# Graph attention and a gated feed-forward net on one core: the edge loop taken out of the scheduler's hands and written in its own order

## The chip, the cores and the metric

The kernel runs on one core of a Trainium2 chip. The core has five engines with a queue each, and each takes its instructions strictly in the order in which the program holds them: TensorE (PE in the profile; its weight loads are a row of their own, PEld), VectorE (DVE), ScalarE (ACT), GpSimd (POOL) and SyncE (SP), which here only starts transfers. Transfers with an index list are started from Pool. The metric is the device time of one execution in microseconds, the median over several; the kernel before has 3848.79 us.

## The reference, cut to what matters

6250 nodes with 256 features, 206,250 edges sorted by their target node `dst`, 64 features an edge. A layer of graph attention with eight heads, then a feed-forward block, then a small mixture of experts, all per node. The part in question is the attention over edges:

```python
q = (x @ Wq.T + bq).reshape(n, HEADS, C)       # k, v likewise
e = (edge_attr @ We.T).reshape(-1, HEADS, C)
k_e = k[src] + e
v_e = v[src] + e
alpha = jnp.sum(q[dst] * k_e, axis=-1) / np.sqrt(C)
amax = jax.ops.segment_max(alpha, dst, num_segments=n)
ex = jnp.exp(alpha - amax[dst])
denom = jax.ops.segment_sum(ex, dst, num_segments=n)
alpha = ex / (denom[dst] + 1e-16)
out = jax.ops.segment_sum(v_e * alpha[..., None], dst, num_segments=n)
...
x = _layernorm(x + h, ln1_g, ln1_b)
h = jax.nn.gelu(x @ W1.T + b1, approximate=False) @ W2.T + b2
return _layernorm(x + h, ln2_g, ln2_b)
```

After it come a gate (softmax, the best two of four experts), four experts and a shared net of three layers, per node, and the sum of them is the output.

## The kernel before

**Stages.** A first stage builds index tables from `dst`. A second computes q, k, v and the skip term for all nodes in 50 blocks of 125 and writes them to `kv_d`, `q_d` and `rn_d` in HBM. Then the edges follow in `sorted_edges`, the branch taken for sorted input; `any_edges` is the branch for other input and does not run here.

**The edge loop.** 403 steps of 512 edges, in four tiles of 128. For step i:
- `load(i)`: four gathers by Pool (line 689) bring the k and v rows of the source nodes into a buffer X, and SP loads the edge features into the same buffer. X has five buffers, and loads are written four steps ahead.
- `score(i)`: TensorE spreads q over the edges (line 705) into two banks `qg`; VectorE multiplies with k (L711) and reduces to one score per head (L713), written into X.
- `turn(i)`: TensorE transposes edge features and scores (L721), ACT copies them out as `xT` (L723).
- `rows(i)`: TensorE multiplies by a small matrix `ws` (L733), which gives scores per target node; VectorE takes their maximum (L737).
- `weigh(i)`: ACT takes the exponentials with that maximum as bias, and their sum (L744).
- `turn_back(i)`: transposes (L752) and a copy `pT` (L754).
- `gather(i)`: sixteen records of products with v and the edge features (L767) into a single bank `op`.
- `keep(i)`: VectorE picks and reduces (L775, L778), ACT copies (L777), SP stores the partial rows `os` to `part_d` (L779).

**Groups.** Every four steps `group(g)` prepares q for four steps: a gather of q rows by Pool (`qq`, L648), a round trip of them through HBM (`qs`, then `qw`, SP), row numbers by SP (`rb`), a comparison on VectorE (`oh`, L671), transposes, products with the edge weights and two copies into `ws` on ACT (L681).

**Nodes.** When all edges of two node blocks are stored, which happens every 16 steps, a generator `ffn(b0, ...)` is appended to `nodes`. It first runs `merge`: four gathers a block by Pool fetch the partial rows (`A`, L788), VectorE joins them (L795 to L821), TensorE applies the edge weights (L825, L832). Then follow the skip gate, a layernorm, the feed-forward block (`h1`, L448 with Gelu L450; `w2`, L459), a second layernorm and the experts (L505 and after). Every `yield` ends a piece. `advance(1)` puts one piece of the first generator into the program; it is called three times in a step.

**What sets the order.** The kernel is written on tiles; a scheduler of the framework orders the instructions of every engine from a cost model of its own and places the waits. The written order is only a priority. One instruction, the load of the scalar table for exponentials behind the Gelus (L451), is pinned to its place. PSUM has eight banks: two for `qg`, two for `m` (transposes and rows), one for `op` and three that turn among groups and nodes.

The loop that writes the steps:

```python
            for i in range(-1 - GQ, B + 2):
                if 0 <= i - 2 < B:
                    keep(i - 2)
                    follow(i - 2)
                if 0 <= i - 1 < B:
                    weigh(i - 1)
                if 0 <= i + 1 < B:
                    score(i + 1)
...
                if 0 <= i + AHEAD < B:
                    load(i + AHEAD)
```

Of the kernel before, what the change touches and what calls it, by code (L numbers as in the profile page):

```python
# [40 lines left out]
def gnn_moe_layer(ctx: ExitStack, tc: tile.TileContext, a: dict, out: bass.AP):  # L41
# [322 lines left out]
    def ffn(b0, p3, bank, attention):  # L364
# [67 lines left out]
        def transposed(v, name):  # L432
            tp = bank([128, 2, M])
            for j in range(n):
                for k in range(2):
                    nc.tensor.transpose(tp[:, k, j * NB : (j + 1) * NB],  # L436
                                        v[:, j, k * 128 : (k + 1) * 128], ident[:NB, :NB])
            vT = p3.tile([128, 2, M], F32, name=name, tag="yT")
            nc.scalar.copy(vT, tp)
            return vT  # L440

        yT = transposed(y, "yT")
# [8 lines left out]
        tc.keep_in_program_order(nc.scalar.preload_act_table_set("natural_log_exp_and_others"))  # L451
# [4 lines left out]
        for j in range(n):  # L456
            ps = bank([NB, D])
            for f in range(FF // 128):
                nc.tensor.matmul(ps, h1[:, f, j * NB : (j + 1) * NB], w2[:, f, :],  # L459
                                 start=(f == 0), stop=(f == FF // 128 - 1))  # L460
                if f == FF // 256 - 1:
# [15 lines left out]
        zT = transposed(z, "zT")  # L477
# [3 lines left out]
        lg = bank([NB, n, NE])  # L481
        for j in range(n):
            for k in range(2):
                nc.tensor.matmul(lg[:, j, :], zT[:, k, j * NB : (j + 1) * NB], gw[:, k, :],  # L484
                                 start=(k == 0), stop=(k == 1))

# [68 lines left out]
        wp = bank([128, NE // 2, M])  # L555
        for j in range(n):
            for g in range(NE // 2):
                nc.tensor.transpose(wp[:, g, j * NB : (j + 1) * NB], wx[:, j, 2 * g : 2 * g + 2].rearrange("p e d -> p (e d)"),
                                    ident[:NB, :NB])
        nc.vector.tensor_tensor(e2, e2, wp, ALU.mult)  # L560
        wt = bank([NE + 1, M])
        for j in range(n):
            nc.tensor.transpose(wt[:, j * NB : (j + 1) * NB], w[:, j, :], ident[:NB, :NB])
        wT = p3.tile([NE + 1, M], F32, name="wT", tag="wT")
        nc.scalar.copy(wT, wt)
        yield
        for j in range(n):
            cs = slice(j * NB, (j + 1) * NB)
            ps = bank([NB, D])
# [3 lines left out]
            nc.tensor.matmul(ps, wT[:, cs], e3b, start=False, stop=True)  # L573
            nc.vector.tensor_tensor(x2[:, j, :], ps, x2[:, j, :], ALU.add)
        yield
        nc.sync.dma_start(rows_of(out), x2)

    def sorted_edges(ctx):
# [50 lines left out]
        with tc.tile_pool(name="fd", bufs=3, space=bass.MemoryType.DRAM) as fd, tc.tile_pool(name="fg", bufs=2) as fg, \  # L629
# [7 lines left out]
                tc.tile_pool(name="f_g", bufs=3, space=PSUM) as f_g:  # L637
            groups = {}
            state = {}

            def bank(shape):
                return f_g.tile(shape, F32, name="gp", tag="gp")

            def group(g):
# [4 lines left out]
                                             in_offset=bass.IndirectOffsetOnAxis(ap=idq[:, g : g + 1], axis=0))  # L649
                yield  # L650
# [14 lines left out]
                yield  # L665
                qw = fg.tile([64, GQ * 2, D], BF16, name="qw")
                for u in range(T // 2):
                    nc.sync.dma_start(qw[32 * u : 32 * u + 3 * W],
                                      qs[64 * u : 64 * (u + 1)].rearrange("(m j) (s d) -> (j s) m d", j=W, s=3))
# [491 lines left out]
```

## Time and profile before

| what | value |
| --- | --- |
| median of 14 runs | 3848.79 us (3832.93 to 3866.11) |
| the profiled execution, its time | 3828.54 us |
| its span, first to last instruction | 3826.8 us |
| granted TensorE clock, mean over the span | 0.763 |
| bytes moved | 727.33 MB, 190 GB/s |
| first score reduce (L713) / last gather product (L767) | 582.9 us / 3692.6 us |

A line of costly groups reads: source line, engine, operation, output and inputs, count, then busy time and mean of one in ns, then the idle time of the engine ahead of these instructions and what ended most of it. A line of waits reads: who waited, for whom, us in total, times, the longest. "issue" stands for time in which nothing that the profile shows was waited for. The clock is given as a share of full speed.

### The profile page before, as it was taken

The page shows a single profiled execution, that of the slowest core. Times are in us where ns is not written, and L with a number is a line of the kernel's source. Part 1 is how long each engine was busy: PE and PEld are TensorE (multiplying, and loading weights), DVE is VectorE, ACT ScalarE, POOL GpSimd, SP SyncE. Part 2 cuts the span into 40 slices and gives each one's busy share as a digit, 9 for nine tenths or more (in the row PEclk, how much of TensorE's full clock was granted, in tenths as well). Part 3 has the DMA queues.
Part 4 walks back from the last instruction along what each step waited for, and adds up shares of the span by engine and source line. Part 5 has one row for each costly group of instructions (what it writes and reads, how often), then busy time and mean ns, then how long its engine had stood idle before and what let it go on. Part 6 is the DMA issues. An engine that isn't in the chain of part 4 may idle for free. (4 is left out here: it accounts for less than half of the span.)

```text
span 3826.8 us, 59098 instructions
## 1 busy us (share of the span) xinstructions
PE 2829.5 (74%) x19362; PEld 1814.8 (47%) x19363; DVE 2401.7 (63%) x5624; ACT 1454.2 (38%) x4313; POOL 1992.7 (52%) x2030
## 2 busy tenths in 40 slices
PE   2566636787777878788888779777878688888866
PEld 2222214454554545455555545554555455555555
DVE  9322225776656756676777567766767677677753
ACT  0111103444434434344444435443434445444442
POOL 0111126766545655656666456655645666567620
PEclk6777767677877777788778867876777778878777
DMA  0233348978667768777878678767866788778730
GB/s 22 102 119 117 116 150 248 269 218 229 199 161 211 208 180 218 218 215 210 229 229 227 179 205 234 219 191 204 234 175 199 223 233 239 200 210 247 221 88 9
DMA packets 611830, 727.33 MB, mean 190 GB/s; under 512 B 384196, under 2 KB 461309, under 8 KB 611514
## 3 DMA queue, kind: packets, MB, share of 16 engines
q0 software_dynamic: 169040, 495.21, 43.7%
q1 hardware_dynamic: 425153, 196.53, 19.8%
q10 hardware_dynamic: 17321, 31.70, 2.3%
q8 instruction: 158, 2.59, 0.3%
q14 instruction: 158, 1.29, 0.1%
HBM read 614.28 MB, written 108.73 MB: 189 GB/s over the span
## 5 line engine op out<-in xcount | busy, mean ns | idle before, releaser
L689 POOL DMA_INDIRECT X<-kv_d,srcT x1612 | 1569.5, 974 | 906.4 <-issue 368.2
L711 DVE TENSOR_TENSOR prod<-qg,X 128x512 f32<-128x512 f32 x806 | 541.3, 682 | 193.1 <-DMA X<-kv_d,srcT 140.5
L713 DVE TENSOR_REDUCE X<-prod 128x32 f32<-128x1024 f32 x403 | 486.6, 1207 | 0.5
L767 PE MATMUL o<-X,pT 128*32 128x192 f32 x6448 | 442.3, 398 | 16.8 <-ACT pT L754 11.6
L705 PE MATMUL qg<-qw,oh 24*128 24x256 bf16 x1612 | 282.2, 314 | 206.8 <-DVE prod L711 193.4
L744 ACT ACTIVATE P<-m,os 128x128 f32<-128x128 f32 x806 | 288.8, 363 | 383.3 <-issue 268.3
L721 PE MATMUL m<-ident,X 128*80 128x128 f32 x1612 | 324.0, 334 | 117.3 <-issue 67.5
L723 ACT COPY xT<-m 80x512 f32<-80x512 f32 x403 | 234.1, 581 | 376.2 <-PE m L721 375.1
L788 POOL DMA_INDIRECT A<-part_d,idp x200 | 255.2, 1276 | 226.3 <-DVE oa L816 102.1
L733 PE MATMUL m<-xT,ws 80*64 80x128 f32 x3224 | 333.9, 336 | 40.7 <-ACT xT L723 37.3
L721 PEld LDWEIGHTS m<-ident,X 128*80 128x80 f32 x1612 | 194.9, 142 | 227.7 <-issue 104.8
L733 PEld LDWEIGHTS m<-xT,ws 80*64 80x64 f32 x3224 | 212.7, 164 | 166.5 <-ACT xT L723 108.1
L752 PE MATMUL m<-ident,P 128*128 128x128 f32 x806 | 208.7, 338 | 88.3 <-ACT P L744 87.5
L767 PEld LDWEIGHTS o<-X,pT 128*32 128x32 f32 x6448 | 194.5, 126 | 165.3 <-issue 69.0
L448 PE MATMUL gp<-yT,w 128*128 128x250 f32 x800 | 236.7, 457 | 41.7 <-ACT h L450 37.0
L737 DVE TENSOR_REDUCE os<-m 128x2 f32<-128x256 f32 x403 | 167.7, 416 | 154.5 <-PE m L733 62.8
L705 PEld LDWEIGHTS <-oh 24*128 24x128 bf16 x1612 | 77.0, 95 | 391.9 <-issue 385.4
L778 DVE TENSOR_REDUCE os<-ov 128x64 f32<-128x256 f32 x403 | 236.6, 587 | 0.1
L299 POOL TENSOR_TENSOR qr<-qt 125x256 f32<-125x256 f32 x50 | 33.4, 669 | 365.0 <-ACT qt L297 345.0
L448 PEld LDWEIGHTS gp<-yT,w 128*128 128x128 f32 x800 | 181.8, 235 | 86.2 <-ACT h L450 40.3
L459 PE MATMUL gp<-w,h 128*125 128x256 f32 x800 | 194.5, 397 | 14.0 <-ACT h L450 13.9
L775 DVE TENSOR_TENSOR ov<-o,hmc 128x256 f32<-128x256 f32 x403 | 167.2, 415 | 54.9 <-PE o L767 54.0
(235 smaller groups left out, 4511.5 us busy)
## 6 DMA issues: line engine op xcount, KB each, us to landing
X<-in_edge_dram SPq DMA_DIRECT2D x403, 128.0 KB
part_d<-os SPq DMA_DIRECT2D x403, 98.0 KB
X<-kv_d,srcT POOLq DMA_INDIRECT x1612
qs<-qq SPq DMA_DIRECT2D x101, 192.0 KB
qw<-qs SPq DMA_DIRECT2D x202, 96.0 KB
q_d<-qt ACTq DMA_DIRECT2D x50, 312.5 KB
rb<-rel_d SPq DMA_DIRECT2D x200, 64.0 KB
rn_d<-rn SPq DMA_DIRECT2D x50, 250.0 KB
```

What stands on the lines that cost most here:

```text
L448: nc.tensor.matmul(ps, w1[:, k, f * 128 : (f + 1) * 128], yT[:, k, :], start=(k == 0), stop=(k == 1))
L689: nc.gpsimd.indirect_dma_start(out=X3[:, t, : 2 * D], out_offset=None, in_=kv_d, in_offset=bass.IndirectOffsetOnAxis(ap=srcT[:, i, t : t + ...
L705: nc.tensor.matmul(qgs[u][:, c, :], oh[rows, 2 * q + c, :], qw[rows, 2 * q + c, :], start=True, stop=True)
L711: nc.vector.tensor_tensor(prod[:, 2 * u : 2 * u + 2, :].rearrange("p t (s c) -> p t s c", s=2), qgs[u].rearrange("p t (s c) -> p t s c", s ...
L713: nc.vector.tensor_reduce(X3[:, :, 2 * D + ED : 2 * D + ED + H], prod.rearrange("p t (h c) -> p t h c", c=C), AX.X, ALU.add)
L721: nc.tensor.transpose(xp[:K, t, :], X3[:, t, 2 * D :], ident)
L723: nc.scalar.copy(xT, xp[:K])
L733: nc.tensor.matmul(sp[(t % 2) * 64 : (t % 2 + 1) * 64, t // 2, :], ws[:, t // 2 * 2 * GQ + 2 * q + t % 2].rearrange("k g w h -> k (g w h)" ...
L744: nc.scalar.activation(P[:, u, :], sp[:, u, :], AF.Exp, bias=os[:, u, PR - 1 : PR], accum_out=os[:, u, PR - 2 : PR - 1])
L767: nc.tensor.matmul(op[32 * r : 32 * (r + 1), u, :].rearrange("p (s c) -> p s c", s=3), pT[:, u, 32 * r : 32 * (r + 1)], va, start=True, st ...
L778: nc.vector.tensor_reduce(os[:, :, 0:C], ov.rearrange("p u h c -> p u c h"), AX.X, ALU.add)
L788: nc.gpsimd.indirect_dma_start(out=A[:, s, i * (H // 2 * PR) : (i + 1) * (H // 2 * PR)], out_offset=None, in_=part_d[: 2 * W * tiles_to(b0 ...
```

## The change

The edge branch gets `tc.manual_schedule()`: inside it every engine's instructions stand in the order in which the program writes them, and the scheduler only places the waits. The loop is rewritten with it:

- `weigh(i)` stands at the end of step i, behind the maximum of `rows(i)`, and no longer at the head of step i + 1.
- `keep` is split. The product and the reduce on VectorE stay at the head of the step; the copy on ACT and the store (`store`) follow the transposes.
- A group runs in six passes and begins seven steps ahead of its first use. All open groups move on by a pass in every step, ahead of `turn`.
- The gathers of partial rows leave `merge` and become `fetch`, begun two steps after the store of the last row needed, two gathers a step, into one buffer for each block of the pair. The node generator is appended six steps later.
- Four pieces of node work a step in place of three; the pieces are cut anew, so that what TensorE writes into a bank is read in the next piece.
- Such banks come from a pool of their own with one buffer, `held`; the turning pool goes from three banks to two.
- The table load behind the Gelus is no longer pinned in this branch. In the other branch both kinds of bank come from one pool of two buffers each.
- The loop runs eight steps longer at its end, without edge work.

```diff
-    def ffn(b0, p3, bank, attention):
+    def ffn(b0, p3, bank, held, attention, pin=True):
...
         def transposed(v, name):
-            tp = bank([128, 2, M])
+            tp = held([128, 2, M])
             for j in range(n):
                 for k in range(2):
                     nc.tensor.transpose(tp[:, k, j * NB : (j + 1) * NB],
                                         v[:, j, k * 128 : (k + 1) * 128], ident[:NB, :NB])
+            yield
             vT = p3.tile([128, 2, M], F32, name=name, tag="yT")
             nc.scalar.copy(vT, tp)
             return vT
...
-        tc.keep_in_program_order(nc.scalar.preload_act_table_set("natural_log_exp_and_others"))
+        ins = nc.scalar.preload_act_table_set("natural_log_exp_and_others")
+        if pin:
+            tc.keep_in_program_order(ins)
...
-            ps = bank([NB, D])
+            ps = held([NB, D])
             for f in range(FF // 128):
                 nc.tensor.matmul(ps, h1[:, f, j * NB : (j + 1) * NB], w2[:, f, :],
                                  start=(f == 0), stop=(f == FF // 128 - 1))
-                if f == FF // 256 - 1:
+                if f % 4 == 3:
                     yield
...
-                tc.tile_pool(name="f_g", bufs=3, space=PSUM) as f_g:
+                tc.tile_pool(name="f_g", bufs=2, space=PSUM) as f_g, \
+                tc.tile_pool(name="f_h", bufs=1, space=PSUM) as f_h, tc.manual_schedule():
...
             def group(g):
...
                                              in_offset=bass.IndirectOffsetOnAxis(ap=idq[:, g : g + 1], axis=0))
                 yield
+                yield
...
                 nc.scalar.copy(qT, tp)
                 yield
+                yield
                 qw = fg.tile([64, GQ * 2, D], BF16, name="qw")
...
+                yield
                 oh = fg.tile([64, GQ * 2, 128], BF16, name="oh")
                 nc.vector.tensor_scalar(oh[:, : 2 * n], rb[:, : 2 * n], j3[:64], None, op0=ALU.is_equal)
-                yield
...
             def keep(i):
-                os, op = state.pop(i)
+                os, op = state[i]
...
+                nc.vector.tensor_reduce(os[:, :, 0:C], ov.rearrange("p u h c -> p u c h"), AX.X, ALU.add)
+
+            def store(i):
+                os, op = state.pop(i)
                 nc.scalar.copy(os[:, :, C : C + ED], op[:, :, 4 * C :])
-                nc.vector.tensor_reduce(os[:, :, 0:C], ov.rearrange("p u h c -> p u c h"), AX.X, ALU.add)
                 nc.sync.dma_start(part_d[2 * W * T * i : 2 * W * T * (i + 1)]
...
-            def merge(b0, n, at):
-                for j in range(n):
-                    A = fm.tile([NB, 2, H * PR], F32, name="A", tag="A")
+            def fetch(b0):
+                rows_of[b0] = []
+                for b in range(b0, min(b0 + 2, NBLK)):
+                    A = fm.tile([NB, 2, H * PR], F32, name="A", tag=f"A{b - b0}")
+                    rows_of[b0].append(A)
                     for s in range(2):
                         for i in range(2):
                             nc.gpsimd.indirect_dma_start(
...
                         yield
-                    for _ in range(4):
-                        yield
+            def merge(b0, n, at):
+                As = rows_of[b0]
+                for j in range(n):
+                    A = As[j]
...
+            def each(steps):
+                for v in list(steps):
+                    if next(v, steps) is steps:
+                        steps.remove(v)
...
-            for i in range(-1 - GQ, B + 2):
-                if i % GQ == GQ - 2 and 0 <= (i + GQ + 2) // GQ < NG or i == -1 - GQ:
-                    prep.append(group(0 if i < -GQ else (i + GQ + 2) // GQ))
+            fetched = []
+            for i in range(-1 - 2 * GQ, B + 10):
+                g, r = divmod(i + 2 * GQ - 1, GQ)
+                if r == 0 and 0 < g < NG or i == -1 - 2 * GQ:
+                    prep.append(group(max(g, 0)))
                 if 0 <= i - 2 < B:
                     keep(i - 2)
-                    follow(i - 2)
-                if 0 <= i - 1 < B:
-                    weigh(i - 1)
                 if 0 <= i + 1 < B:
                     score(i + 1)
+                each(prep)
                 if 0 <= i < B:
                     turn(i)
                 if 0 <= i - 1 < B:
                     turn_back(i - 1)
+                if 0 <= i - 2 < B:
+                    store(i - 2)
                 advance(1)
                 if 0 <= i < B:
                     rows(i)
                 advance(1)
                 if 0 <= i - 1 < B:
                     gather(i - 1)
+                if 0 <= i < B:
+                    weigh(i)
+                advance(1)
                 if 0 <= i + AHEAD < B:
                     load(i + AHEAD)
-                for g in prep[:1]:
-                    if next(g, prep) is prep:
-                        prep.pop(0)
+                fetched += [fetch(b0) for b0 in after(i - 4)]
+                each(fetched)
+                nodes += [ffn(b0, p3, bank, held, merge, pin=False) for b0 in after(i - 10)]
                 advance(1)
             advance(1000)
```

`after(i)` yields the pairs whose last partial row belongs to step i.

## The prediction

> **What bounds the kernel now.** I read the page's busy shares and its 40 slices first, then the costly groups and the waits by engine, then five-microsecond windows through one stall and its timeline, and last the tail.
>
> ```profile
> PE 2829.5 (74%) x19362; PEld 1814.8 (47%) x19363; DVE 2401.7 (63%) x5624; ACT 1454.2 (38%) x4313; POOL 1992.7 (52%) x2030
> L689 POOL DMA_INDIRECT X<-kv_d,srcT x1612 | 1569.5, 974 | 906.4 <-issue 368.2
> L788 POOL DMA_INDIRECT A<-part_d,idp x200 | 255.2, 1276 | 226.3 <-DVE oa L816 102.1
> ```
>
> No engine is full. Pool's gap in front of a gather is 0.30 us where it waits for nothing (368.2/1208), so one costs 0.95 + 0.30 = 1.25 us and a step's four 5.0; with a quarter of a q gather a step needs 5.3 us of Pool at least. The tile's waits and the waits of VectorE say who holds the loop up:
>
> ```profile
> PE qg L705 <- DVE prod L711: 193.4, 121, 12.5
> DVE A L795 <- DMA A<-part_d,idp: 144.8, 22, 10.9
> POOL A L788 <- DVE oa L816: 102.1, 8, 23.0
> DVE t L407 <- DMA rn<-rn_d: 92.9, 11, 12.5
> DVE oh L671 <- DMA rb<-rel_d: 64.4, 13, 14.7
> ```
>
> Three loads (A, rn, rb) arrive late behind an instruction that stands early in VectorE's order: 144.8 + 92.9 + 64.4 = 302 us in which VectorE stands still, and TensorE (qg) and Pool after it. One such stall, in windows (busy of PE, PEld, DVE, ACT, POOL; granted clock, DMA share, GB/s) and in the timeline:
>
> ```profile
> 2115.00:2120.00 5.00, 0.85 (x5) 0.31 (x5) 2.13 (x5) 1.67 (x5) 2.26 (x3) 0.69 1.00 278
> 2120.00:2125.00 5.00, 0.00 (x0) 0.00 (x0) 0.69 (x1) 0.00 (x0) 0.00 (x0) 0.50 0.53 154
> 2125.00:2130.00 5.00, 1.55 (x5) 0.98 (x5) 2.89 (x7) 0.00 (x0) 0.00 (x0) 0.50 0.16 41
> ...
> 2135.00:2140.00 5.00, 5.00 (x29) 4.02 (x28) 3.36 (x9) 1.65 (x4) 0.00 (x0) 1.00 0.00 0
> ```
>
> ```profile
> 2127.00 0.48 DVE L671 TENSOR_SCALAR oh<-rb,j 64x1024 bf16<-64x1024 bf16 x1 [2.28 <-DMA rb<-rel_d]
> 2128.45 0.58 PE L705 MATMUL qg<-qw,oh 24*128 24x256 bf16 x2 [11.88 <-DVE prod L711]
> 2142.16 0.94 POOL L689 DMA_INDIRECT X<-kv_d,srcT  x1 [24.29 <-DVE ln_st L390]
> ```
>
> Everything is dark for 10 us, the clock falls to 0.50, and Pool gets no free X buffer for 24 us. The starts of the 403 reduces L713 in the timeline give the pace: 582.9 for the first, 32 steps to 769.5 (5.83 us each, hardly any node work yet), then 890.2 to 3649.8 for steps 48 to 400, which is 7.84 us a step or 125.4 us per 16 steps, the interval at which node pairs become ready. 44 steps over 13 us hold 833 us. The last gather product ends at 3692.6; the tail is then 134 us.
>
> **The change, part by part.** *Order.* The work is the same; what changes is who stands behind whom. I add up 16 steps (one node pair) by the written order. Start to start in the timeline, a step's edge work is 3.7 us on VectorE (product 2 x 0.61, reduce 1.13, kept rows 0.33 + 0.51, maximum 0.34, the small ones 0.2), and 2.9 us on TensorE at full clock (q 0.35, transposes 0.45 + 0.32, rows 0.59, gather product 0.79, a quarter of the group's 1.6). VectorE and TensorE can drift apart by less than a step (ov needs the last gather product, which needs the ov before it), so the dearer engine sets each step. Four pieces of the node generator fall into a step, 51 pieces in all, so 13 of 16 steps carry some.
> - Merge and layernorm, six steps: pieces of 3.7, 0.3, 3.4, 1.0, 4.8 and 3.9 us on VectorE (512-wide 0.60, 256-wide 0.34, dependent small ones 0.2) make steps of 7.4, 4.3, 7.1, 5.7, 8.5 and 7.6: the fourth adds 1.0 for the transposes that gather waits behind. 40.6 us.
> - Three steps with h1 and w2: the yT transposes 1.1; edge work up to rows 1.1; h1 whole 7.3 (32 records at 0.23, as 16 of L505 took 3.55); rows 0.6, w2 quarter 1.75, gather 0.8, quarter 1.75; then 1.1, 1.75, 0.6, 1.75, 0.8; then VectorE 1.4 + 7.7 and transposes 1.1. With hops about 29.7 us.
> - Four steps of gate and experts, TensorE: 7.7, 7.3, 5.4, 5.0 = 25.4. Pool has to issue four steps of 5.3 plus the next pair's eight A gathers at about 1.55, 33.6 us. An X buffer is filled three steps ahead of its product, so Pool may fall some 8 us behind here; without that cover the step's sum grows by 8.
> - Three steps without node work at Pool's 5.3: 16.
>
> Together 111.7 at full clock.
>
> *The exponentials* (two of 0.36 + 0.20, 0.8 in all) move from the head of step i+1 to the tail of step i. Behind them wait the dense copies of the fourth slot; they were not on the path of the step, and TB(i) a step later has over 2 us in hand: nothing. If that slack is gone, 0.8 a step. *Scalar tables*: 67 + 25 + 23 + 20 = 135 loads of 1.283 become about 50, since Gelu stands in one piece; 85 x 1.28 = 109 us of ACT, an engine at 38%, and I count nothing for it beyond the h1 piece, which no longer waits for them.
> *q groups over six passes*: qs, qw and oh stand two passes behind the DMA that feeds them, some 14 us against landings of about 5 to 8 (qq 7.5 at most to its transpose); oh's 64.4 goes. The two ws copies (2 x 0.62) now stand in ACT's queue ahead of xT in one step of four, and rows waits for xT: 1.2 x 4, half of it in steps that TensorE sets: +2.
> *Partial rows early*: 200 gathers, same number, issued six steps before their merge and into two buffers: 144.8 and Pool's 102.1 go. rn is loaded five steps ahead of its use, now in order: 92.9 goes.
> *Banks*: the turning pool falls from three to two and one bank is held. In h1 a bank is free when Gelu (0.47) and two hops are done, before the next pair of products (0.92) ends: nothing; if not, about 0.5 a product, 4 us per pair.
> [...] If each of the eight products waited out its Gelu, 8 x 0.65 x 25 = 130 us would come on top; no such wait stands in this trace, with three banks.
>
> *Clock.* 16 gather products take 0.86 us at full clock and 1.51 in the slow stretches, so work at half clock costs 0.75 more. L767's mean of 398 ns between 349 and 531 (its median and maximum over 890 to 3650) puts about 27% of the work there now. Steps that VectorE sets leave TensorE idle half the time, so the slow share will not vanish, but the dark stretches go. From both sides: 46 us of TensorE work on the path x 0.75 x 0 to 27% is 0 to 9; I take 12%, +4.
> [...]
>
> **Sum.** 111.7 + 2 + 4 = 118 us per 16 steps. First reduce 583; the first pair enters ten steps later than its rows, so 35 steps at 5.8 = 203; 23 sixteens x 118 = 2714; last steps 13. Tail: the last pair but one has hardly begun (before it was about there too); a pair alone takes 57.5 from 3769.4 to the end and two merges of 9, 76 us; 71 + 76 = 147. Total 583 + 203 + 2714 + 13 + 147 = 3660 in the profiled execution's terms. That execution was 3828.54 (span 3826.8), 20 below the median of 3848.79: 3680.
>
> **The rivals.**
> *A. All waits go and the order costs nothing* (fast): 3828 - 302 = 3526, as a median 3545. For it: from the first reduce to the last are 3093 us, so the other 358 steps average (3093 - 833)/358 = 6.3 us, with node work in them. Against it: the pieces come whole, h1 and half of w2 in one step of 14 us, which a finer mixture avoids.
> *B. Half clock in the heavy pieces* (slower than before). Place: h1 and w2 come right behind two steps of 8 us in which TensorE has 3 us of work, the condition under which windows show 0.50. Price: 46 x 0.75 = 35 us per pair if all of it ran so; at half, 111.7 + 2 + 17 = 131, 946 + 23 x 131 = 3959, median 3980. It decides from 125.3 us per pair, a slow share of a third. Against it: in the windows of 600 to 700, with TensorE two thirds busy, the clock was 0.82.
> *C. Pool takes the place.* Its eight A gathers in four steps are not hidden and the products wait for X: 118 + 8 = 126, 3844, median 3865: next to no change. Against it: three steps of lead, and a Pool that idles in the nine steps before.
> *D. The order isn't what sets the pace*, and part of the stalls moves to X's landing: prod waits 140.5 us for it now; as much again gives 3660 + 140 = 3800, median 3820.
>
> **Numbers.** Forecast (3560 to 3770) 0.60; A or faster 0.16; D 0.08; C 0.05; B 0.11. One can tell 0.3%, 12 us, from no change. Faster is 0.60 + 0.16 + 0.08 less 0.02 of D, whose upper end reaches the border: 0.82. Same is that 0.02 and 0.02 of C: 0.04. Slower is B and the rest of C: 0.14. The range leaves out half of A and nearly all of B: 3490 to 3860.
>
> **What would show it.** VectorE's waits for A, rn and rb near zero; table loads about 50; POOL A no longer waiting for oa; no step over 20 us, one of 13 to 17 per pair; 16 steps in 112 to 123 us; clock over 0.78. It is wrong if qg still waits over 100 us for prod, if rows waits for ws copies over 100 us, or if prod waits over 250 us for X.

## The result, and the profile after

The changed kernel takes 4142.23 us (median of 10 runs, 4130.13 to 4162.67) against 3844.94 us for the kernel before beside it (47 runs): a ratio of 1.0777 with a 95% interval of 1.0752 to 1.0801. It is slower by 7.8%, where 3680 us and "faster" had been predicted. The profiled execution took 4149.3 us, its span is 4147.5 us and the mean granted clock 0.722 (before: 3826.8 us, 0.763).

The span divides as the prediction's sum does, which shows where the miss lies:

| part of the sum | predicted | after |
| --- | --- | --- |
| start to the first reduce | 583 | 577.6 |
| the next 35 steps | 203 | 192.8 |
| the remaining 367 steps | 2714 | 3218.2 |
| last reduce to the end | 160 | 158.9 |

Everything around the loop with node work was right to a few us. Per 16 steps the loop takes 140 us (steps 48 to 400: 139.8), not 118, and 125.4 before. Without node work (the first 32 steps) a step is now 5.3 us, 0.5 less than before.

The engine shares of the changed kernel, then its costly groups and its tile and DMA waits, in the columns explained earlier:

```profile
PE 2862.4 (69%) x19362; PEld 1837.8 (44%) x19363; DVE 2517.8 (61%) x5624; ACT 1344.8 (32%) x4229; POOL 1955.8 (47%) x2030
```

```profile
L704 POOL DMA_INDIRECT X<-kv_d,srcT x1612 | 1548.0, 960 | 1452.7 <-PE o L782 999.1 <-issue 375.4 <-DMA X<-kv_d,srcT 11.2
L449 PE MATMUL gp<-yT,w 128*128 128x250 f32 x800 | 192.5, 396 | 24.7 <-ACT h L451 23.4 <-ACT yT L440 1.3
L782 PE MATMUL o<-X,pT 128*32 128x192 f32 x6448 | 465.3, 421 | 24.4 <-ACT os L796 24.3
```

```profile
POOL X L704 <- PE o L782: 999.1, 187, 18.7
DVE os L752 <- PE m L748: 336.6, 121, 8.0
DVE prod L726 <- PE qg L720: 228.8, 135, 7.2
PE qg L720 <- DMA qw<-qs: 226.1, 74, 11.8
PE gh L436 <- DVE y L429: 159.1, 25, 10.0
PE m L748 <- ACT xT L738: 140.8, 258, 2.0
PE gh L436 <- DVE y L400: 137.0, 25, 6.3
DVE os L752 <- DMA part_d<-os: 125.4, 23, 8.5
PE gp L676 <- DMA qq<-q_d,idq: 89.6, 30, 9.7
```

The most telling number is TensorE's busy time: 2862.4 us against 2829.5, only 33 us more, in a span that grew by 321. TensorE idles 4147.5 - 2862.4 = 1285 us in place of 997. Against the kernel before, then, nearly all of the lost time is waiting and not slower work. The waits for A, rn and rb are gone from VectorE, as predicted; in their place TensorE waits for qw (226 us, 12 before) and for the node values y (296 us, 36 before), and VectorE for the rows (337 us, 63 before). The wait for qq (90 us) was there before (87). Pool's 999 us in front of the X gathers are a symptom: it waits until the gather products have freed an X buffer, so it is ahead of the loop and not what holds it up.

A node pair now takes the same course every time. The intervals between the reduces L728 from step 208 on, in us, show one pair:

```
10.1 4.2 3.8 10.0 7.5 7.5 4.2 14.2 7.7 9.0 8.8 18.2 6.4 8.7 11.7 7.9
```

The 14.2 is a stall that nearly every pair has; over steps 48 to 400 this step takes 13.1 us on average. In the windows (busy of PE, PEld, DVE, ACT, POOL; clock, DMA share, GB/s) and the timeline of the changed kernel:

```profile
2205.00:2210.00 5.00, 0.00 (x0) 0.00 (x0) 0.70 (x4) 0.25 (x1) 2.41 (x3) 0.50 0.95 284
2210.00:2215.00 5.00, 3.85 (x20) 2.39 (x19) 4.86 (x12) 1.94 (x8) 0.00 (x0) 0.50 0.55 160
...
2245.00:2250.00 5.00, 5.00 (x24) 4.11 (x24) 0.00 (x0) 2.54 (x6) 0.00 (x0) 1.00 0.00 0
```

```profile
2191.42 6.95 SPq L683 DMA_DIRECT2D qw<-qs  x2
2198.48 7.15 SPq L797 DMA_DIRECT2D part_d<-os  x1
2209.23 0.43 DVE L752 TENSOR_REDUCE os<-m 128x2 f32<-128x256 f32 x1 [6.72 <-DMA part_d<-os]
2210.70 1.09 PE L720 MATMUL qg<-qw,oh 24*128 24x256 bf16 x4 [8.95 <-DMA qw<-qs]
...
2219.40 0.94 POOL L704 DMA_INDIRECT X<-kv_d,srcT  x1 [11.38 <-PE o L782]
...
2237.08 1.10 PE L436 MATMUL gh<-ident,y 125*128 125x125 f32 x4 [5.92 <-DVE y L429]
```

From 2190 to 2210 the DMA engines' share is 0.88 to 1.01 in windows of 5 us. In that time SyncE needs 6.95 us to issue the two qw copies and then 7.15 us for one store. The q rows arrive after 2210, TensorE stands for 8.95 us in front of its q products with other work written behind them, and VectorE for 6.72 us. At 2237 TensorE stands again, this time for y. In the third window h1 occupies TensorE for 5 us, VectorE does nothing and no DMA runs: one engine is full and ScalarE works 2.54 us, while VectorE, Pool and the DMA are dark.

### The profile page after: what moved, and what is told of

It reads as the page before. It is cut to its first block, busy times and chain, and to the rows that moved or that the text cites. A ratio compares the mean times of both kernels' runs of the same rounds, so it can differ in the third digit from the quotient of the medians.

```text
span 4147.5 us, 59038 instructions
## 1 busy us (share of the span) xinstructions
PE 2862.4 (69%) x19362; PEld 1837.8 (44%) x19363; DVE 2517.8 (61%) x5624; ACT 1344.8 (32%) x4229; POOL 1955.8 (47%) x2030
## 5 line engine op out<-in xcount | busy, mean ns | idle before, releaser
L704 POOL DMA_INDIRECT X<-kv_d,srcT x1612 | 1548.0, 960 | 1452.7 <-PE o L782 999.1
L726 DVE TENSOR_TENSOR prod<-qg,X 128x512 f32<-128x512 f32 x806 | 519.3, 683 | 273.0 <-PE qg L720 228.8
L728 DVE TENSOR_REDUCE X<-prod 128x32 f32<-128x1024 f32 x403 | 491.7, 1220 | 13.9
L782 PE MATMUL o<-X,pT 128*32 128x192 f32 x6448 | 465.3, 421 | 24.4 <-ACT os L796 24.3
L752 DVE TENSOR_REDUCE os<-m 128x2 f32<-128x256 f32 x403 | 169.3, 420 | 463.3 <-PE m L748 336.6
L720 PE MATMUL qg<-qw,oh 24*128 24x256 bf16 x1612 | 229.0, 337 | 262.2 <-DMA qw<-qs 226.1
L736 PE MATMUL m<-ident,X 128*80 128x128 f32 x1612 | 338.9, 349 | 3.5 <-PE qg L720 2.6
L436 PE MATMUL gh<-ident,y 125*128 125x125 f32 x200 | 55.0, 430 | 296.1 <-DVE y L429 159.1
L736 PEld LDWEIGHTS m<-ident,X 128*80 128x80 f32 x1612 | 217.2, 150 | 81.0 <-PE o L782 37.6
L720 PEld LDWEIGHTS <-oh 24*128 24x128 bf16 x1612 | 61.6, 98 | 409.5 <-issue 372.8
L449 PE MATMUL gp<-yT,w 128*128 128x250 f32 x800 | 192.5, 396 | 24.7 <-ACT h L451 23.4
L462 PE MATMUL gh<-w,h 128*125 128x256 f32 x800 | 195.6, 388 | 1.0 <-DVE t L466 1.0
```

Source lines behind the costliest of these rows:

```text
L449: nc.tensor.matmul(ps, w1[:, k, f * 128 : (f + 1) * 128], yT[:, k, :], start=(k == 0), stop=(k == 1))
L704: nc.gpsimd.indirect_dma_start(out=X3[:, t, : 2 * D], out_offset=None, in_=kv_d, in_offset=bass.IndirectOffsetOnAxis(ap=srcT[:, i, t : t + ...
L720: nc.tensor.matmul(qgs[u][:, c, :], oh[rows, 2 * q + c, :], qw[rows, 2 * q + c, :], start=True, stop=True)
L726: nc.vector.tensor_tensor(prod[:, 2 * u : 2 * u + 2, :].rearrange("p t (s c) -> p t s c", s=2), qgs[u].rearrange("p t (s c) -> p t s c", s ...
L728: nc.vector.tensor_reduce(X3[:, :, 2 * D + ED : 2 * D + ED + H], prod.rearrange("p t (h c) -> p t h c", c=C), AX.X, ALU.add)
L736: nc.tensor.transpose(xp[:K, t, :], X3[:, t, 2 * D :], ident)
```

## The experiments

Each kernel ran beside the kernel before on the same chip, and the ratio is made with that. Those of this table ran on one chip, in three sittings in which the kernel before took 3856.59, 3857.59 and 3859.73 us; the change's line is the comparison told above, with 3844.94 us for the kernel before. "16 steps" is read from the timeline as in the prediction; TensorE's idle time is the span of the profiled execution less TensorE's busy time in it.

| kernel | median us | ratio to before (95%) | 16 steps | TensorE idle |
| --- | --- | --- | --- | --- |
| before | 3856.59 | 1 | 125.4 | 997 |
| the change | 4142.23 | 1.0777 (1.0752 to 1.0801) | 139.8 | 1285 |
| groups two steps earlier | 4039.42 | 1.0469 (1.0403 to 1.0535) | 135.3 | 1262 |
| scheduler's order | 3783.74 | 0.9816 (0.9763 to 0.9868) | 124.4 | 932 |
| h1 two pieces later | 4104.54 | 1.0657 (1.0595 to 1.0719) | 137.8 | 1286 |
| eight os buffers | 4128.67 | 1.0707 (1.0650 to 1.0764) | 140.0 | 1281 |
| fill ahead of transposes | 4119.48 | 1.0666 (1.0619 to 1.0713) | 138.3 | 1133 |
| early groups, late transposes | 3964.41 | 1.0274 (1.0195 to 1.0352) | 131.9 | 1218 |
| before in written order | 4514.21 | 1.1695 (1.1646 to 1.1745) | 152.4 | 1522 |
| scheduled, two qq | 3790.19 | 0.9829 (0.9787 to 0.9871) | 123.8 | 928 |
| score behind rows | 4177.03 | 1.0855 (1.0796 to 1.0914) | 139.9 | 1195 |
| score two ahead | 4023.70 | 1.0469 (1.0408 to 1.0531) | 134.1 | 1238 |
| scheduled, early groups | 3894.24 | 1.0096 (1.0062 to 1.0131) | 128.5 | 1032 |

With the fill, its 177 us of products count as busy.

**Early q rows.** The groups begin two steps earlier.

```diff
-            for i in range(-1 - 2 * GQ, B + 10):
-                g, r = divmod(i + 2 * GQ - 1, GQ)
+            for i in range(-3 - 2 * GQ, B + 10):
+                g, r = divmod(i + 2 * GQ + 1, GQ)
```

> The changed kernel with every q group begun two steps earlier, so that qw is issued four steps ahead of its use in place of two; nothing else differs. Theory Q (late q rows are the larger part of the loss): TensorE's waits for qw (226 us) and qq (107 and 90 on its two rows) fall below 60 together, the pattern of 16 steps loses its 14.4 and 10.0 and falls from 139.8 to about 125, time 3800 to 3880. Theory C (the half clock and the steps set by VectorE are the larger part): the waits go, but the time stays above 4000, since other waits fill the place. Theory S (SP's queue is blocked by its own issues of up to 8.7 us, wherever they stand): qw's wait goes, the 125 us of waits for the store part_d stay, 3950 to 4050.

The time fell to 4039.42 us, 2.9% below the change by the two ratios. TensorE's wait for qw left the list, the step of the stall fell from 13.1 to 9.0 us on average, and 16 steps fell by 4.5 us. So the lead that I had given the q rows was too short, but this is a third to two fifths of the loss and not the whole: theory C fits, not Q. The wait for qq stayed (104 us), and VectorE's wait for X rose from 39 to 174 us. One line of its waits shows what else stays, the node transposes' wait for y:

```profile
PE gh L436 <- DVE y L429: 161.8, 25, 10.1
```

**The order given back to the scheduler.** All other parts of the change stay.

```diff
-                tc.tile_pool(name="f_h", bufs=1, space=PSUM) as f_h, tc.manual_schedule():
+                tc.tile_pool(name="f_h", bufs=1, space=PSUM) as f_h:
...
-                nodes += [ffn(b0, p3, bank, held, merge, pin=False) for b0 in after(i - 10)]
+                nodes += [ffn(b0, p3, bank, held, merge, pin=True) for b0 in after(i - 10)]
```

> The changed kernel without the manual schedule (the table load pinned again); passes, early fetch, pieces, banks and four pieces a step are kept, and the scheduler orders the engines. If the written order itself makes the loss: not slower than before, 3700 to 3860, with VectorE's waits for A, rn and rb mostly gone. If banks and pieces make it (two turning banks, one held): over 3950 with long waits for gp or gh banks.

3783.74 us, 8.9% below the change and 1.8% below the kernel before. That separates the two halves of the change on this chip: the written order (with the loose table load) costs some 360 us, the parts beside it gain some 70. They were to remove 302 us of VectorE's waits; the waits of this kernel show where most of it went:

```profile
POOL qq L661 <- PE gp L676: 238.1, 22, 11.3
DVE prod L726 <- DMA X<-kv_d,srcT: 235.1, 119, 5.1
DVE A L819 <- DMA A<-part_d,idp: 117.5, 24, 8.6
```

VectorE's wait for X grew from 140.5 to 235.1 us and 117.5 of the 144.8 for A are back. The scheduler moves `fetch` too: the last gather of a block's partial rows is issued 8.0 us ahead of their merge (median), against 29.3 us in the change.

**The place of h1.**

```diff
         yT = yield from transposed(y, "yT")
         yield
+        yield
+        yield
```

> The changed kernel with two empty pieces in front of h1, which moves h1 from between transposes and rows to behind gather and the exponentials of the step. Theory H (the whole h1 piece in front of rows and gather starves Pool and VectorE): Pool's wait for gather (999 us) falls by 150 or more, the 18.1 us step falls to about 12, time 3990 to 4050. Theories Q and C: a step of 16 to 18 us stays somewhere, time within 40 us of 4142.

4104.54 us: 1.1% below the change, within the 40 us of theories Q and C. The step of h1 fell from 18.2 to 15.5 us on average, not to 12. Pool's wait for the gather products did fall, by 222 us to 777, as theory H had it, but the time did not follow; TensorE's wait for qq doubled to 182 us.

**Store buffers.** VectorE's 6.72 us in front of L752 are put down to the store that must free os.

```diff
-                tc.tile_pool(name="fo", bufs=4) as fo, \
+                tc.tile_pool(name="fo", bufs=8) as fo, \
```

> The changed kernel with eight buffers for the kept rows os in place of four. Theory S: the 125 us in which the maximum waits for the store part_d are a wait of their own, time 4020 to 4060. Theories Q and C: they lie under the wait for qw in the same step, the wait goes and the time stays within 30 us of 4142.

4128.67 us, and 140.0 us per 16 steps: no gain in the loop, though the wait for the store is gone. It lay in the shadow of TensorE's wait for qw, which ends 1.5 us later in the timeline above.

**Is it the clock?** TensorE is kept busy while it waits for y.

```diff
             tp = held([128, 2, M])
+            for _ in range(24):
+                nc.tensor.transpose(tp[:, 0, 0:NB], ident[:NB, :], ident[:NB, :NB])
```

> 24 extra transposes of the identity go to TensorE directly ahead of the node transposes of y and z (L436), into the same bank, which the real ones then overwrite; they need nothing that is late, so TensorE works through most of the 5.9 and 5.4 us for which it waits there in each node pair. Theory 'half clock behind an idle stretch': the 50 stretches of low clock behind those waits (some 5 to 8 us of work each at 0.5 in place of 1.0) shrink, the L782 mean falls from 421 ns to about 400, the wait gh<-y (296 us) falls to under 120, and the time falls by 40 to 120 us, to 4020 to 4100. Rival 'the waits themselves, the clock follows the load and not the place': 4142 within 20, or later where the extra transposes (3 to 7 us each time, 50 times) run over the arrival of y: up to 4250.

4119.48 us, 1.0% below the change. Its groups:

```profile
L435 PE MATMUL gh<-ident 125*128 125x125 f32 x1200 | 177.1, 317 | 2.1 <-DVE at L861 1.0 <-DVE t L468 1.0
L438 PE MATMUL gh<-ident,y 125*128 125x125 f32 x200 | 41.3, 320 | 120.7 <-DVE y L400 68.2 <-DVE y L429 52.5
L451 PE MATMUL gp<-yT,w 128*128 128x250 f32 x800 | 189.7, 391 | 33.2 <-ACT h L453 31.9 <-ACT yT L442 1.3
L784 PE MATMUL o<-X,pT 128*32 128x192 f32 x6448 | 462.5, 419 | 26.4 <-ACT os L798 26.4
```

The wait shrank from 296 to 121 us and the real transposes ran at 320 ns in place of 430, but h1 behind them stays at 391 ns (396) and the gather products at 419 (421), not the 400 expected. By the ratios the gain is at the low end of what the theory gave. It speaks for these two places only: in the two steps of the fill the granted clock rose from 0.50 to 0.79 and from 0.66 to 0.89, while h1's step had 0.94 already and the steps of merge and gate kept their low clock (0.52 to 0.68 in four of them). What the slow clock costs there wasn't tried. In windows of 5 us from 1000 to 4000 us of the changed kernel, one behind a window with under 2 us of TensorE work had a granted clock of 0.51 on average (103 windows), one behind over 4.5 us of work 0.88 (257 windows); in the kernel before, from 1000 to 3600 us, 0.53 (48) and 0.90 (260). So in these windows the clock mostly went with the load just before; yet 43 of the 257 were under 0.60, and in the kernel before TensorE was busy for 22.59 of the 25 us from 705 to 730 at a clock of 0.50. The averages do not say what the clock is worth: with 40% of the gather products slow, by the prediction's reckoning, against 27% before, TensorE's total work grew by 33 us, as others ran faster (h1's products took 396 ns, 457 before, and 192.5 us in place of 236.7).

**Both late inputs at once.** Groups two steps earlier, and two more yields ahead of each of the two `transposed`.

```diff
+        yield
+        yield
         yT = yield from transposed(y, "yT")
...
+        yield
+        yield
         zT = yield from transposed(z, "zT")
```

> The groups begin two steps earlier (as in the first experiment, 4039) and the node transposes of y and z are issued two pieces later, so that h1 also comes two pieces later (alone 4104). Theory 'every late input stalls a whole engine because the order is fixed': both savings add, and the 296 us for which TensorE waits for y go to under 100; 16 steps fall from 135.3 to about 126 and the time to 3850 to 3950. Rival 'the wait moves on to the next input': gh<-y goes, but X<-o, prod<-X or P<-os take it up, and the time stays at 4000 to 4050.

3964.41 us. The savings add (1.0777 - 0.031 - 0.012 = 1.035 from the first and third run alone, 1.0274 measured), yet the time ends between the two theories: y's waits fell to 43 + 13 us, and others grew.

```profile
DVE os L756 <- DMA part_d<-os: 109.6, 22, 8.9
DVE prod L730 <- PE qg L724: 392.7, 115, 7.9
ACT P L763 <- DVE os L756: 352.3, 156, 8.8
```

One place is left that can be named: the step of the old stall still takes 12.2 us on average, and in it VectorE now waits 5.0 us for the store that frees os, with TensorE behind it for the exponentials (5.7 us). The wait for qw that covered this is gone. Eight os buffers weren't tried on this kernel, so what the wait costs here is not known.

**The kernel before in written order**, with nothing else of the change than the loose table load.

```diff
-        tc.keep_in_program_order(nc.scalar.preload_act_table_set("natural_log_exp_and_others"))
+        nc.scalar.preload_act_table_set("natural_log_exp_and_others")
...
-                tc.tile_pool(name="f_g", bufs=3, space=PSUM) as f_g:
+                tc.tile_pool(name="f_g", bufs=3, space=PSUM) as f_g, tc.manual_schedule():
```

> The kernel before with its edge loop in written order and nothing else changed: no scheduler, no wait of the five that the change's other parts remove is taken away. Theory 'the order costs, the other parts gain': with the order by the scheduler the other parts took 3845 to 3784 (2%); so written order without them costs more than the 9% that it costs with them: 4300 to 5000. TensorE waits for VectorE and the DMA queues in every node step, the clock falls under 0.70. Rival 'the new placement of the parts is what hurts in written order': the kernel before in written order is not above 4142.

4514.21 us. Written order costs 17% on the old loop; the change's own placing earns 9 of these points back. The clock fell to 0.69 to 0.71, not clearly under the 0.70 expected. Its waits:

```profile
POOL X L689 <- PE o L767: 1048.0, 206, 14.9
PE m L752 <- ACT P L744: 535.9, 280, 21.1
PE gp L662 <- DMA qq<-q_d,idq: 429.9, 87, 15.9
```

The exponentials stood at the head of the next step, and TensorE waited 536 us for them; the change puts them behind the maximum, and it waits 17 us for them there (87.5 us in the kernel before, with the scheduler).

**Two q buffers under the scheduler**: `qq` from the pool with two buffers.

> All parts of the change but with the scheduler's order, as in the second experiment (3784), and two buffers for the gathered q rows (qq). There Pool waited 238 us in 22 waits of 10.8 us until the transposes had read the one buffer, and VectorE 235 us for X behind it. Theory 'Pool's wait makes X late': both waits fall by half or more and the time falls to 3680 to 3760. Rival 'X is late by the bandwidth of its gathers': the qq wait goes, prod<-X stays above 180, time 3784 within 20.

3790.19 us, no change. The time and the wait for X are as the rival had them, but the qq wait is still there: the scheduler uses the second buffer to begin the group sooner (the gather is issued 58 us ahead of its transposes, median, in place of 22).

```profile
DVE prod L726 <- DMA X<-kv_d,srcT: 251.7, 135, 5.6
POOL qq L661 <- PE gp L676: 232.2, 24, 11.3
```

**Another order inside the step.** On top of "early groups, late transposes", first `score` of the next step behind `rows`, then `score` two steps ahead. In the second kernel groups also begin one step earlier, so that `rows` of the last step of each group of four reads row weights (`ws`, two buffers) already overwritten for a later group: it does the same amount of work on wrong values, and its time counts only as such.

```diff
-                if 0 <= i + 1 < B:
-                    score(i + 1)
...
                 if 0 <= i < B:
                     rows(i)
+                if 0 <= i + 1 < B:
+                    score(i + 1)
```

> The kernel with early groups and late transposes (3964, 1.0274) with one more edit: score of the next step is issued behind rows in place of ahead of turn, so that VectorE's maximum os no longer stands behind prod and its reduce, and the exponential P follows sooner. In that kernel ScalarE waited 352 us for os and TensorE 201 us for P. Theory 'short chains inside a step': both fall under half and the time falls to 3880 to 3930. Rival 'the wait moves': turn of the next step now stands close behind the reduce that it needs, TensorE waits for it in most of 403 steps (0.3 to 1 us each), 3940 to 4100.

> As the run before, but score runs two steps ahead in place of one (groups one step earlier too), so that the maximum is ahead of prod and the reduce has a whole step until turn needs it. X is used one step sooner behind its load (two steps in place of three). Theory 'short chains inside a step': waits for os, P and the reduce all fall, 3800 to 3900. Rival 'X becomes late': VectorE waits over 300 us for X, 3950 or more.

4177.03 and 4023.70 us, both slower than 3964. The waits for os by the exponentials fell to about half (352 to 180 and 192 us), as the theory had it, but the maximum itself now waits. Of the first of the two:

```profile
DVE os L756 <- PE m L752: 909.5, 329, 10.6
```

In the first the edge-only steps went from 5.4 to 6.1 us, and the loss is slower work: TensorE is busy for 2975 us in place of 2756 (gather products 445 ns, 415 before) and idles 24 us less. With score two ahead X was not late as the rival had it (170.9 us, over 300 expected); the maximum's wait was 627 us there. In both, moving one operation in a written order moved the wait and gained nothing.

**Early groups under the scheduler.**

> All parts with the scheduler's order (3784, 0.9816) and the groups begun two steps earlier, as in the first experiment. Theory 'late q rows cost only where the order is fixed': the scheduler sends other work ahead while q rows are on their way, 3784 within 20. Rival 'they cost in both': 3700 to 3760.

3894.24 us, 2.9% slower than without the edit, where both theories had excluded a loss. The same edit gained 2.9% in written order. VectorE's wait for A doubled:

```profile
DVE A L819 <- DMA A<-part_d,idp: 234.7, 25, 12.3
```

Pool starts every gather (in the changed kernel 1612 for X, 200 for A and 101 for q rows, none of which overlaps the next), so one that is issued earlier stands ahead of others; that this is the reason wasn't tried.

**h1 in four pieces**, on top of "early groups, late transposes".

```diff
             nc.scalar.activation(h1[:, f, :], ps, AF.Gelu, bias=b1c[:, f : f + 1])
+            if f % 2 == 1 and f < FF // 128 - 1:
+                yield
```

> The kernel with early groups and late transposes (3964, 1.0274) with h1 issued in four pieces of two blocks in place of one of eight (three more yields, so that a node pair takes three pieces more and keeps a few to spare in its 16 steps). Its three steps around h1 take 11.3, 8.1 and 13.0 us there (32.4). Theory 'a coarse piece holds up the edge work of the whole step behind it': these steps and the next become 7 to 9 us each, and the time falls by 25 x 4 to 8 us, to 3770 to 3870. Rival 'the pieces only shift': the same TensorE work and the same waits lie in other steps, 3964 within 30.

4151.09 us, but on a chip on which the kernel before takes 4176.73: 0.9941 (0.9919 to 0.9963). That could not be set beside 1.0274, so four kernels ran together, on a third chip (before: 4182.99 us).

> Early groups, late transposes and h1 in four pieces once more, now on one chip with the three kernels beside it. Theory 'the coarse h1 piece holds up a step': the ratio to the change with the first two edits alone is 0.96 to 0.98. Rival 'the chip made it': 0.99 to 1.01.

> Early groups and late transposes alone, the partner of the run before: 1.0274 of before on the first chip. If the ratio differs by over 0.02 on this one, ratios of different chips can't be compared at all.

> The change with h1 in four pieces as its one edit. Theory 'the coarse h1 piece holds up a step': the two steps of 17 to 18 and 8.8 us around h1 become three of 8 to 10, 16 steps fall by 4 to 8 us and the time by 80 to 180 us. Rival 'it shifts the other waits, or the q rows that are late anyway decide': within 30 us of the change.

> The change as it stands, as the base of the three runs on the same chip: 1.0777 of before if the ratio carries from chip to chip.

| kernel | median us | ratio to before (95%) | ratio to the change |
| --- | --- | --- | --- |
| the change | 4364.02 | 1.0429 (1.0401 to 1.0457) | 1 |
| h1 in four pieces alone | 4262.63 | 1.0202 (1.0168 to 1.0236) | 0.977 |
| early groups, late transposes | 4156.73 | 0.9931 (0.9905 to 0.9957) | 0.953 |
| all three | 4167.75 | 0.9971 (0.9953 to 0.9989) | 0.955 |

The change's wait for qw on this chip, where TensorE waits 5 us for qq and VectorE 12 us for the store:

```profile
PE qg L720 <- DMA qw<-qs: 26.9, 16, 5.6
```

On the first chip these waits were 226, 90 and 125 us. So the late q rows cost little here; without them the change is still 4.3% slower than the kernel before, and TensorE idles 1414 us. The two edits gain here mainly by y, whose wait falls from 276 to 42 us.

The ratio of the two edits differs by 0.034 from that on the first chip, more than the 0.02 set as the bound. Of the three edits the rival won: the pieces bring 2.3% alone and nothing where the late inputs are mended. The ratio of these two written kernels is nearly the same on both chips (0.953 here, 3964.41 / 4142.23 = 0.957 on the first), though not the same waits went; the ratio to the scheduled kernel isn't: 1.043 and 1.078.

The four pieces alone saved 101 us, as the theory of the coarse piece had it; with the other edits the time is the same within 11 us.

So the scheduled kernel ran once more, on a fourth chip (before: 4137.68 us), with h1 in one piece and in four.

> All parts with the scheduler's order once more, on whichever chip this is. Theory 'the gain is of the parts': 0.97 to 0.99 of the kernel before, here as on the first chip. Rival 'it is of that chip': 0.99 to 1.02.

> All parts with the scheduler's order, and h1 in four pieces. Theory 'under the scheduler the place of a piece is not decisive, its own readiness is': within 1% of the same kernel with h1 in one piece, beside it. Rival 'smaller pieces help here too': 0.96 to 0.985 of it.

One piece: 4148.92 us, 1.0008 (0.9977 to 1.0039); four pieces: 4068.28 us, 0.9833 (0.9784 to 0.9881). The rival expectation held both times: the gain of 1.8% over the kernel before is not of the parts alone, and smaller pieces help the scheduler by 1.9%. The version to keep is all parts without written order and h1 in four pieces; on the one chip on which it ran it was 1.7% below the kernel before and 1.9% below the scheduled kernel with h1 in one piece (the change itself did not run there).

## Why the prediction was wrong

- **The step that failed** is the one headed "Order": "the dearer engine sets each step", a sum of durations with hops (handovers from engine to engine) priced only inside h1. In written order an engine that waited held up what was written behind it, so a step was the dearer engine plus what the others made it wait for. In the stall at 2210 TensorE started nothing for the 8.95 us in front of its q products, and VectorE, itself held in front of the maximum, worked 0.70 of the 5 us from 2205 on. In the changed kernel's trace the instructions of the edge loop start on every engine in the order in which they are written, with small exceptions: on VectorE L544 starts 0.02 us ahead of L543 in 23 of 25 pairs, and on TensorE two q products (L720) start ahead of the last record of L579 in 23 places. With all other parts the same, TensorE idles 1285 us in written order and 932 us in the scheduler's, at nearly equal work (2862 and 2849 us): 353 us that the sum doesn't have. The two pairs of runs with the order exchanged (and the pin of the table load with it) show its price: 1.0777 against 0.9816 with the new parts, 1.1695 against 1 with the old.
- **"q groups over six passes"** held the largest wait for a transfer, and I had counted it as covered. It set 14 us of lead against landings of 5 to 8, an estimate of mine (the longest wait for qq in the trace before was 7.5 us). The copies' issue alone took 6.95 us on SyncE, and TensorE waited 226 us for qw. Two steps more of lead were worth 2.9% on the first chip; on the third the wait hardly occurs. The trace before held issues of these copies of up to 9.7 us, and I had counted the landings without them. The stall that the prediction shows has one, with the late rb loads behind it in SyncE's queue:

```profile
2110.16 10.30 SPq L668 DMA_DIRECT2D qw<-qs  x2
2120.51 1.49 SPq L657 DMA_DIRECT2D rb<-rel_d  x2
```

- **The steps by size.** Against the per-step sum of 111.7 the trace has 139.8 (averages over steps 48 to 400). The first, second and fifth step of merge and layernorm are nearly right (7.5, 4.7, 9.1 against 7.4, 4.3, 8.5), the fourth and sixth took 8.1 and 8.8 for 5.7 and 7.6. The third has 13.1 for 7.1 (qw), the three h1 steps 33.2 for 29.7, gate and experts 34.7 for 25.4, the edge-only steps 20.7 for 16. The terms listed for the h1 steps add up to 30.6 before any hop, so 29.7 was too low by itself.
- **Clock.** I took 12% of the work as slow; by the same reckoning the trace has about 40% (gather products at a mean of 421 ns). At the prediction's own price that is 46 x 0.75 x 0.40 = 14 us a pair in place of 4, so up to 10 of the 22 us that a pair took too long. It shows in the four steps of gate and experts: TensorE is busy for 31.9 of their 34.7 us, for work counted as 25.4, at a clock of 0.66, 1.00, 0.75 and 0.99. How much of this lay on the path, no run shows. Rival B, which gave 3980, had the sign right and the share nearly (a third decides, it said), but not the place: h1 and the step behind it ran at 0.94 and 1.00, the slow work stood in merge and layernorm (0.50 to 0.61 in four steps) and in the gate. Nor does it explain the loss against the kernel before, where TensorE's work grew by 33 us in all. That it came nearest is in part luck.
- **What was right.** The waits for A, rn and rb went; the loop's table loads fell from 135 to 51 (about 50 predicted); Pool's wait for oa went from 131 (102.1 of it in the line shown) to 19 us; the start, the first 35 steps and the tail were right; prod waits 39 us for X. No step was over 20 us, but the clock was 0.722 where over 0.78 was named. Of the signs named for being wrong, rows waits 141 us for xT (37 before), though not only behind the ws copies, while qg's wait for prod fell from 193 to 7 us and gave way to the one for qw. But the 302 us did not come back as time: under the scheduler the parts gained about 70 us on the first chip and nothing on the fourth. On the first, VectorE's wait for X grew, as rival D described; on the fourth no wait for X is left and there is still no gain, so that is not the whole reason.
- **Still open.** From 3964 to 3784 us the one place that can be named is the store's wait above; its price wasn't measured. Two more orders of the step were slower, a finer h1 brought nothing. That the two orders differ in hundreds of small waits is argued, not shown.

## What to carry to other kernels

Before writing an order by hand, price each input's arrival against its place under the load of the new loop, not the old: add to the dearer engine every hop that nothing written behind it can cover. Run "order alone" and "parts alone" as two kernels first; on the first chip they had opposite signs. Compare TensorE's idle time and its busy time, both: the first tells waiting, the second slower work. Compare kernels on the same chip only, and where two edits overlap, try the second again on top of the first.

## What the hardware showed that I had not expected

- Issuing a DMA from SyncE took up to 8.7 us in the changed kernel (qw; 9.7 in the kernel before); the store of partial rows took 7.15 us at 2198 and 0.36 us at 2222. What is queued behind it on SyncE is issued later: that store began 0.11 us after the two qw issues of 6.95 us had ended, and none of SyncE's 1517 issues in the changed kernel overlaps the next. Of the 202 qw issues 46 took over 2 us, 2 in the kernel before, and none with the same parts in the scheduler's order, which moved more bytes a second (192 GB/s against 175). So busy DMA engines alone don't explain it; the reason is open.
- The kernel before took 3857 us on one chip and 4138 to 4183 on three others, 7 to 8% more. In the edge-only stretch the changed kernel's granted clock was 0.72 on the first chip and 0.60 on the third, with TensorE busy for about 106 of 140 us in both. The window of the changed kernel on the first chip, then on the third:

```profile
600.00:740.00 140.00, 105.03 (x973) 62.20 (x971) 104.41 (x190) 58.09 (x204) 105.89 (x112) 0.72 0.96 283
```

```profile
620.00:760.00 140.00, 107.94 (x810) 64.02 (x811) 87.04 (x159) 49.36 (x171) 87.17 (x93) 0.60 0.82 229
```

At about equal busy time the second did 810 products where the first did 973. Why that chip grants less is not known from these runs.
